# Chosen-token lists written by indirect stores to DRAM, and early sums tied to a point of each half tile

## The chip, the cores and the metric

The kernel runs on one core of a Trainium2 chip. Five engines of the core run their own instruction streams in order: TensorE (PE in the profile, with PEld for its weight loads), VectorE (DVE), ScalarE (ACT), GpSimd (POOL) and SyncE (SP). SP issues most DMAs, POOL issues the indirect ones. An instruction that waits holds up all that stand behind it on the same engine, and so does a DMA that cannot yet be issued. The metric is the device time of one execution in microseconds (us); before the change it is 5029.28 us, the median of three runs (5026.99 to 5029.7).

## What is computed

```
x = x + ssm(layernorm(x))                       # 8 sequences of 2048 tokens, 512 wide
h = layernorm(x)
light = window attention over h                 # 64-token windows and their neighbours
s   = h . routing_token                         # one score per token, for queries and for keys
scores = coordinate_descent(s, 50 iterations)   # then top_k: 512 queries, 1024 keys a sequence
out = null_q everywhere; out[chosen queries] = heavy attention(chosen queries, chosen keys)
x = x + light + out
```

The choice of tokens is a list of row numbers and one weight for each entry: per sequence 512 query rows and 1024 key rows. The order inside a list is not in the result, only which row goes with which weight.

## The kernel before

**Three phases.** `ssm_phase` computes the state space model and stores its result to DRAM (`ys`). `light_phase` makes x1 (input plus that result), its norm, the window attention, and the routing scores. `heavy_phase` gathers the chosen rows with indirect DMAs and does the full attention over them. The chip is most of the time in the last two.

**Tiling of the light phase.** There are 128 tiles of 128 tokens (`NTT`), taken in 32 macro tiles of four (`NMT`, index n). Each tile is done in two half tiles of four heads, so `steps()` (lines 930 to 1000) runs 256 half-tile steps s. A step turns the weights of step s (`turned`, L885 to L892), finishes the tile before it (`finish`, L912 to L919) or runs a piece of the projections of the next macro tile (`front`, L790 to L808), weighs step s+2 (`weigh`, L859 to L875), and sums (`sum_up`, L903 to L907). PE's order is that of the program text (a manual schedule). The other engines' orders are made by a scheduler from the dependences and the order of recording; `tc.issue_after(i)` keeps what is recorded under it from being placed before instruction i.

**Finishing a tile.** DVE adds the projection and x1 into `row` (L914); SP stores `row` to `base` (L916); POOL adds the null query into `nul` (L918); SP stores `nul` to the output (L919). `row` and `nul` have two buffers each, so the row of tile t can be written only when POOL has read the row of tile t-2 and SP's store of it is done. x1 for a tile comes back from DRAM as `x1r` (L944), three buffers, issued by SP two tiles ahead. POOL also copies the halo of `xt` (L766) and `kk` (L785) once per macro tile.

**Sums and scores.** `total` loads x (L673), gathers the state space result in reverse order with an indirect DMA on POOL (L678), adds (L682) and takes the mean and variance. `score` stores x1 (L703) and forms the two routing scores (L709); `scale` multiplies them by the root (L719). For the first 16 macro tiles (`FIRST`) this is done in `rows(n)`, two macro tiles ahead of use; for the last 16 in `early(n)`, spread over the first 16 macro tiles as `sooner`, one piece at the end of every step, with no anchor.

**Routing.** `route` is a generator per group of four sequences. `between` advances each running one by one piece, twice a step, with its instructions anchored behind those of the step. It does 49 iterations of the descent, 33 halvings of a threshold, and a running count, which gives each chosen token its place in its list (`r_u`) and leaves 1,000,000 (`SKIP`) for the others. Then the list is built by products: for each of the eight lists of the group, DVE makes selection matrices (`r_ge`, `r_at`, `r_dat`, and `r_one` at L591), PE multiplies them (L597, 128x128 by 128x16, four in a piece) and DVE adds up (`r_acc`, L600 and L602) and writes the row numbers `ix` and the weights `wt`. Group 0 starts at n = 15, group 1 at n = 16. The heavy phase reads group 0's lists first and group 1's half way.

Of the kernel before, what the change touches and what calls it, by code (L numbers as in the profile page):

```python
# [17 lines left out]
P = 128  # L18
# [362 lines left out]
N_BISECT = 33  # L381
SKIP = 1.0e6
NLT = NKV // P


def route_consts(tc, k, pool):
    nc = tc.nc

    k.before = pool.tile([P, P], F32, name="before", tag="before")
    nc.gpsimd.memset(k.before, 1.0)  # L390
    sv = k.before.rearrange("p (r t) -> p r t", t=NCK)
    nc.gpsimd.affine_select(sv, sv, [[-NCK, P // NCK], [0, NCK]], ALU.is_ge, 0.0, base=0,
                            channel_multiplier=1)
# [12 lines left out]
    k.na1 = pool.tile([P, 1], F32, name="na1", tag="na1")  # L406
    k.num = pool.tile([P, 1], F32, name="num", tag="num")
    for r, (keff, n) in enumerate(((KEFF_Q, NQ), (KEFF_KV, NKV))):
        s = slice(64 * r, 64 * r + 64)
        nc.vector.memset(k.logk[s], math.log(keff))  # L410

        nc.vector.memset(k.na1[s], math.log(L) - math.log(keff))
        nc.vector.memset(k.num[s], float(n))

    k.tiles = pool.tile([P, NLT + 1], F32, name="tiles", tag="tiles")
    nc.gpsimd.iota(k.tiles, [[P, NLT + 1]], base=0, channel_multiplier=0,
                   allow_small_or_imprecise_dtypes=True)
    k.places = pool.tile([P, P], F32, name="places", tag="places")
    nc.gpsimd.iota(k.places, [[1, P]], base=0, channel_multiplier=0,
                   allow_small_or_imprecise_dtypes=True)  # L420


def route(tc, k, ps, gi, ix, wt):

# [143 lines left out]

    NA = 4
    for rb in range(2 * GB):
        cs = slice(rb * NCK, (rb + 1) * NCK)
        rs = slice(rb % GB * NCK, (rb % GB + 1) * NCK)
        ge = pool.tile([P, NCK, NLT + 1], F32, name="r_ge", tag=f"r_ge{gi}", bufs=1)
        nc.vector.tensor_tensor(ge, pos[:, cs].unsqueeze(2).to_broadcast([P, NCK, NLT + 1]),
                                k.tiles.unsqueeze(1).to_broadcast([P, NCK, NLT + 1]), ALU.is_ge)
        at = pool.tile([P, NCK], F32, name="r_at", tag=f"r_at{gi}", bufs=1)  # L580
        nc.vector.reduce_sum(at, ge[:, :, 1:], axis=AX.X)
        nc.vector.scalar_tensor_tensor(at, at, -float(P), pos[:, cs], ALU.mult, ALU.add)
        dat = pool.tile([P, NCK, 2, NLT], F32, name="r_dat", tag=f"r_dat{gi}", bufs=1)
        nc.vector.tensor_tensor(dat[:, :, 1], ge[:, :, :NLT], ge[:, :, 1:], ALU.subtract)
        for e, src in ((0, rows[:, rs]), (1, wts[:, cs])):
            nc.vector.tensor_tensor(dat[:, :, e], dat[:, :, 1],
                                    src.unsqueeze(2).to_broadcast([P, NCK, NLT]), ALU.mult)
        acc = pool.tile([P, 2, NLT], F32, name="r_acc", tag=f"r_acc{gi}", bufs=2)
        for i in range(0, NCK, NA):
            one = pool.tile([P, NA, P], F32, name="r_one", tag=f"r_one{gi}", bufs=1)  # L590
            nc.vector.tensor_tensor(one, at[:, i : i + NA].unsqueeze(2).to_broadcast([P, NA, P]),  # L591
                                    k.places.unsqueeze(1).to_broadcast([P, NA, P]),
                                    ALU.is_equal)
            yield
            pa = pst((P, 2, NLT))
            for j in range(NA):
                nc.tensor.matmul(pa, one[:, j, :], dat[:, i + j], start=j == 0,  # L597
                                 stop=j == NA - 1)
            if i == 0:
                nc.vector.tensor_copy(acc, pa)  # L600
            else:
                nc.vector.tensor_tensor(acc, acc, pa, ALU.add)  # L602
        nc.vector.tensor_copy(ix[:, rb], acc[:, 0])
        nc.vector.tensor_copy(wt[:, rb], acc[:, 1])

# [7 lines left out]
def light_phase(tc, k, ps, wp, args, x, ys, x1, base, out, between, after):  # L613
# [6 lines left out]
    with ExitStack() as ctx:  # L620
        k.pool = ctx.enter_context(tc.tile_pool(name="route", bufs=1, reuse_waits="tile"))
        route_consts(tc, k, k.pool)
        scores = k.scores = [k.pool.tile([P, P], F32, name=f"sc{i}", tag=f"sc{i}")
                             for i in range(B // GB)]
        cst = ctx.enter_context(tc.tile_pool(name="li_c", bufs=1, reuse_waits="tile"))
# [43 lines left out]
        def total(n, i):  # L669

            c = n * MT + i
            t = sb.tile([P, D], F32, name="x1t", tag="x1t", bufs=6)
            nc.sync.dma_start(t, xf[c * P : (c + 1) * P, :])  # L673
            y = sb.tile([P, D], F32, name="yt", tag="yt", bufs=2)
            b, r = divmod(c, NCK)

            with tc.issue_after(came["pow"].ins) if n == 1 else nullcontext():
                nc.gpsimd.indirect_dma_start(  # L678
                    out=y, out_offset=None, in_=ys[b],
                    in_offset=bass.IndirectOffsetOnAxis(ap=back[:, r : r + 1], axis=0),  # L680
                    bounds_check=L - 1, oob_is_err=False)
            nc.vector.tensor_add(t, t, y)  # L682
            st = sb.tile([P, 6], F32, name="st", tag="st", bufs=3)
            nc.vector.bn_stats(st, t)
            nc.vector.bn_aggr(mv[:, c, :], st)
            return t

        def roots(n):
# [8 lines left out]
                                    ALU.mult, ALU.add)  # L697
            came["pow"] = nc.gpsimd.tensor_tensor(rc[:, :, ns], rc[:, :, ns], k.halves, ALU.pow)

        def score(n, i, t):  # L700

            r0 = (n * MT + i) * P
            nc.sync.dma_start(x1[r0 : r0 + P, :], t)  # L703
# [9 lines left out]
        def scale(n):  # L713

            b, c = divmod(n * MT, NCK)
            for r in range(2):
                col = (r * GB + b % GB) * NCK + c
                sc = scores[b // GB][:, col : col + MT]
                nc.vector.tensor_tensor(sc, sc, rc[:, 0, n * MT : (n + 1) * MT], ALU.mult)  # L719

        def early(n):

            for i in range(MT):
                t = total(n, i)
                yield
                score(n, i, t)
                yield
            roots(n)
            scale(n)

        def rows(n):
# [11 lines left out]
            for i in range(MT):  # L743
                c = n * MT + i
                if n >= FIRST:
                    t = sb.tile([P, D], F32, name="x1t", tag="x1t", bufs=6)
                    nc.sync.dma_start(t, x1[c * P : (c + 1) * P, :])
                    ts.append(t)
                nc.vector.tensor_scalar(z[:, i, :], ts[i], mv[:, c, 0:1], rc[:, 1, c : c + 1],
                                        ALU.subtract, ALU.mult)  # L750
                if n < FIRST:
                    score(n, i, ts[i])
                yield
            if n < FIRST:
                scale(n)
            it["z"] = z

# [175 lines left out]
        def steps():  # L933
# [20 lines left out]

            for s in range(2):
                weigh(s)
            ahead = beyond = turning = sooner = None
            done = None
            for s in range(nst):
                t, half = divmod(s, 2)  # L960
# [378 lines left out]
def model(ctx, tc, ins, out, debug=None):  # L1339
# [9 lines left out]
    if debug is not None:  # L1349
# [6 lines left out]
    wp = ctx.enter_context(tc.tile_pool(name="wts", bufs=1, reuse_waits="tile"))  # L1356
    lists = [[rpool.tile([P, 2 * GB, NLT], dt, name=f"{n}{i}", tag=f"{n}{i}")
              for n, dt in (("ix", U32), ("wt", F32))] for i in range(B // GB)]
    running = []

    def between(anchors=None, group=None):


        if group is not None:
            running.append(route(tc, k, ps, group, *lists[group]))
            return
        for r in list(running):
            with ExitStack() as held:
# [46 lines left out]
```

## Time and profile before

| what | value |
|---|---|
| median of three runs | 5029.28 us |
| the profiled execution's own time | 5022.05 us |
| its span | 5020.4 us |
| mean granted TensorE clock | 0.972 |
| busy share PE / DVE / ACT / POOL | 91% / 59% / 38% / 17% |
| state space phase | to about 541 us |
| light phase | to about 3305 us |
| heavy phase | from there to the end |

The span is the time between the first and the last instruction of one profiled execution. A group's row in the profile names the line, the engine, the tiles written and read, the shape and how often it occurs; then the busy time in us and the mean of one in ns; then the engine's idle time just before the group and what ended it. A busy row of PE counts matmuls whose ends are modelled, so rows of different groups can overlap and their sum can exceed the time. One float32 matmul of the program stands in the profile as two.

### The profile page before, as it was taken

The page shows a single profiled execution, that of the slowest core. Times are in us where ns is not written, and L with a number is a line of the kernel's source. Part 1 is how long each engine was busy: PE and PEld are TensorE (multiplying, and loading weights), DVE is VectorE, ACT ScalarE, POOL GpSimd, SP SyncE. Part 2 cuts the span into 40 slices and gives each one's busy share as a digit, 9 for nine tenths or more (in the row PEclk, how much of TensorE's full clock was granted, in tenths as well). Part 3 has the DMA queues.
Part 4 walks back from the last instruction along what each step waited for, and adds up shares of the span by engine and source line. Part 5 has one row for each costly group of instructions (what it writes and reads, how often), then busy time and mean ns, then how long its engine had stood idle before and what let it go on. Part 6 is the DMA issues. An engine that isn't in the chain of part 4 may idle for free. (4 is left out here: it accounts for less than half of the span.)

```text
span 5020.4 us, 75066 instructions
## 1 busy us (share of the span) xinstructions
PE 4572.1 (91%) x28808; PEld 2684.0 (53%) x28808; DVE 2946.8 (59%) x7240; ACT 1892.5 (38%) x5077; POOL 852.8 (17%) x878
## 2 busy tenths in 40 slices
PE   0867689999999999999999999989999999999987
PEld 0656445555555555555555565545555555555554
DVE  8566586767676655666677655444444444444443
ACT  6967223333333333444333222323333333333333
POOL 6344231222222110000000000020111011110000
PEclk9988799999999999999999999999999999999998
DMA  7487642334333321111111101220000000010000
GB/s 258 145 234 234 207 156 93 129 101 137 102 125 105 103 76 47 55 53 55 49 53 51 45 32 37 59 87 22 30 26 30 18 26 30 26 30 18 20 9 13
DMA packets 286344, 392.48 MB, mean 78 GB/s; under 512 B 38304, under 2 KB 152224, under 8 KB 285984
## 3 DMA queue, kind: packets, MB, share of 16 engines
q1 hardware_dynamic: 241056, 278.59, 16.9%
q0 software_dynamic: 29840, 101.73, 6.6%
q10 hardware_dynamic: 15088, 7.34, 0.5%
q8 instruction: 227, 3.72, 0.3%
q14 instruction: 133, 1.09, 0.1%
HBM read 244.46 MB, written 143.13 MB: 77 GB/s over the span
## 5 line engine op out<-in xcount | busy, mean ns | idle before, releaser
L790 PE MATMUL pp<-xt,wqkv 128*128 128x512 f32 x2048 | 952.8, 609 | 11.7 <-DVE kk L795 11.7
L790 PEld LDWEIGHTS pp<-xt,wqkv 128*128 128x128 f32 x2048 | 375.5, 193 | 421.0 <-issue 407.3
L869 ACT ACTIVATE pe<-sim,nb 128x256 f32<-128x256 f32 x1024 | 471.1, 473 | 239.2 <-DVE nb L864 163.1
L1215 DVE TENSOR_REDUCE mx<-sim 128x1 f32<-128x1024 f32 x256 | 312.8, 1222 | 339.8 <-PE sim L1209 192.7
L803 PE MATMUL pv<-wqkv,xt 128*128 128x512 f32 x1032 | 472.6, 601 | 0.0
L912 PE MATMUL pr<-wo,ot 128*128 128x512 f32 x1024 | 460.8, 593 | 0.0
L1219 ACT ACTIVATE pe<-sim,nb 128x1024 f32<-128x1024 f32 x256 | 285.3, 1114 | 457.0 <-DVE nb L1216 444.2
L907 ACT COPY ot<-po 128x256 f32<-128x256 f32 x256 | 95.3, 372 | 918.8 <-PE po L903 917.5
L864 DVE TENSOR_REDUCE nb<-sim 128x4 f32<-128x1024 f32 x256 | 311.7, 1217 | 137.1 <-PE sim L859 130.3
L918 POOL TENSOR_TENSOR nul<-row,nq 128x512 f32<-128x512 f32 x128 | 168.7, 1318 | 1256.6 <-DVE row L914 948.9
L1284 PE MATMUL pt<-ident,pe 128*128 128x128 f32 x2048 | 283.1, 282 | 87.9 <-ACT pe L1219 61.3
L1158 PE MATMUL pp<-xt,wa 128*128 128x512 f32 x768 | 351.8, 602 | 4.4 <-DVE kk L1163 4.4
L1284 PEld LDWEIGHTS pt<-ident,pe 128*128 128x128 f32 x2048 | 232.0, 144 | 171.2 <-ACT pe L1219 88.2
L1287 DVE COPY pw<-pt 128x512 f32<-128x512 f32 x256 | 175.5, 685 | 242.6 <-PE pt L1284 242.1
L885 PEld LDWEIGHTS pt<-ident,pe 128*128 128x128 f32 x2048 | 239.8, 141 | 132.0 <-issue 131.1
L903 PE MATMUL po<-pw,v 128*64 128x128 f32 x4096 | 292.1, 285 | 15.0 <-DVE pw L892 14.6
L875 DVE TENSOR_SCALAR pe<-pe,rec 128x256 f32<-128x256 f32 x1024 | 300.3, 355 | 6.0
L803 PEld LDWEIGHTS pv<-wqkv,xt 128*128 128x128 f32 x1032 | 185.6, 189 | 204.7 <-issue 200.1
L912 PEld LDWEIGHTS pr<-wo,ot 128*128 128x128 f32 x1024 | 184.6, 190 | 183.8 <-issue 183.3
L1289 ACT COPY pw<-pt 128x512 f32<-128x512 f32 x256 | 149.8, 585 | 350.5 <-PE pt L1284 350.5
L903 PEld LDWEIGHTS po<-pw,v 128*64 128x64 f32 x4096 | 224.4, 139 | 84.3 <-issue 48.9
L1209 PE MATMUL sim<-kk,q 64*128 64x512 f32 x1024 | 267.0, 641 | 0.0
(241 smaller groups left out, 7019.1 us busy)
## 6 DMA issues: line engine op xcount, KB each, us to landing
xin<-in_L_attn_x_dram SPq DMA_DIRECT2D x32, 1024.0 KB, 5.6
toe<-kd SPq DMA_DIRECT2D x64, 512.0 KB, 3.9
x1t<-in_L_attn_x_dram SPq DMA_DIRECT2D x128, 256.0 KB, 2.9
x<-x1t SPq DMA_DIRECT2D x128, 256.0 KB, 2.2
x1r<-x SPq DMA_DIRECT2D x128, 256.0 KB, 2.8
base<-row SPq DMA_DIRECT2D x128, 256.0 KB, 2.1
out_dram<-nul SPq DMA_DIRECT2D x128, 256.0 KB, 2.1
y<-xb POOLq DMA_DIRECT2D x25, 1024.0 KB, 11.0
```

The lines of the kernel that those rows point to most:

```text
L790: nc.tensor.matmul(pp, wqkv[:, c, j * D + f * P : j * D + (f + 1) * P], xt[:, c, WIN:], start=c == 0, stop=c == NC - 1)
L803: nc.tensor.matmul(pv[0:m], xt[:, c, s * P : s * P + m], wqkv[:, c, 2 * D :], start=c == 0, stop=c == NC - 1)
L864: dve = nc.vector.reduce_max(nb, sim.rearrange("p a b c -> p (a b) c"), axis=AX.X, negate=True)
L869: act = nc.scalar.activation(pe[:, i, :], sim[:, i // 2, i % 2, :], AF.Exp, bias=nb[:, i : i + 1], accum_out=sums[:, i : i + 1])
L875: nc.vector.tensor_scalar(pe[:, i, :], pe[:, i, :], rec[:, i : i + 1], None, ALU.mult)
L903: nc.tensor.matmul(po[64 * par : 64 * par + 64, pr, :], vs[kb][:, h * DH : (h + 1) * DH], self.pw[pr][:, par, kb, :], start=kb == 0, stop= ...
L912: nc.tensor.matmul(pr, ot[:, c, :], wo[:, c, :], start=c == 0, stop=c == NC - 1)
L1158: nc.tensor.matmul(pp, w[:, f * P : (f + 1) * P], xt[:, c, :], start=c == 0, stop=c == NC - 1)
L1209: nc.tensor.matmul(sim[:, par, ms], q[rows_, f, self.qs], kk[rows_, f, ms], start=True, stop=True)
L1215: nc.vector.reduce_max(mx, sim[:, par, :], axis=AX.X, negate=True)
L1219: nc.scalar.activation(pe, sim[:, par, :], AF.Exp, bias=self.nb[:, h : h + 1], accum_out=self.sums[:, h : h + 1])
L1284: nc.tensor.transpose(pt[:, i, :], pes[half][:, kb * P : (kb + 1) * P], k.ident)
```

## The change

**Lists.** The products are gone. Each list position gets the list's first slot added (`k.first`), is cast to an integer (`r_to`), and row number and weight are put side by side (`r_pair`). For each of the 128 columns (eight lists by 16 tiles) an indirect store on POOL writes 128 pairs of 8 bytes to DRAM at their places; places beyond the bound are dropped. The columns go in turn to four DRAM copies of the lists (`NFL`), which were filled with zeros at the start of the light phase. SP then loads the four copies of each list back (`r_got`), and DVE sums them (`r_one`) and writes `ix` and `wt`. The generator yields after every second store. Group 0 starts one macro tile sooner, at n = 14.

**Early sums.** The pieces of `sooner` stand under `issue_after` of the first instruction that `turned` returned, in the middle of the step. The x1 store is taken out of `score` and issued ahead of it. The scores of the first two macro tiles are left out of `rows` and done by `later` at n = 2 and 3, from x1 loaded again. `scale` runs on POOL in place of DVE. `x1t` has seven buffers in place of six, `yt` three in place of two.

```diff
+NFL = 4
...
-    k.tiles = pool.tile([P, NLT + 1], F32, name="tiles", tag="tiles")
...
+    k.first = pool.tile([P, 2 * GB, NCK], F32, name="first", tag="first")
+    nc.gpsimd.iota(k.first, [[NKV, 2 * GB], [0, NCK]], base=0, channel_multiplier=0,
...
-    NA = 4
-    for rb in range(2 * GB):
...
-            one = pool.tile([P, NA, P], F32, name="r_one", tag=f"r_one{gi}", bufs=1)
-            nc.vector.tensor_tensor(one, at[:, i : i + NA].unsqueeze(2).to_broadcast([P, NA, P]),
...
+    nc.vector.tensor_tensor(pos, pos, k.first, ALU.add)
+    nc.vector.tensor_copy(to, pos)
+    nc.vector.tensor_copy(pair[:, :, 1], wts)
+    for r in range(2):
+        nc.vector.tensor_copy(pair[:, r * GB * NCK : (r + 1) * GB * NCK, 0], rows)
+    yield
+    for b in range(GB):
+        for rb, n in ((b, NQT), (GB + b, NLT)):
+            for c in range(rb * NCK, (rb + 1) * NCK):
+                nc.gpsimd.indirect_dma_start(
+                    out=flat[c % NFL], out_offset=bass.IndirectOffsetOnAxis(ap=to[:, c : c + 1],
+                                                                            axis=0),
+                    in_=pair[:, c, :], in_offset=None, bounds_check=2 * GB * NKV - 1,
+                    oob_is_err=False)
+                if c % 2:
+                    yield
+    for b in range(GB):
+        for rb, n in ((b, NQT), (GB + b, NLT)):
+            got = pool.tile([P, NFL, NLT, 2], F32, name="r_got", tag=f"r_got{gi}", bufs=2)
+            with nc.allow_non_contiguous_dma(reason="pairs"):
+                for i in range(NFL):
+                    nc.sync.dma_start(
+                        got[:, i, :n], flat[i][rb * NKV : rb * NKV + n * P, :].rearrange(
+                            "(t p) e -> p t e", p=P))
             yield
-            pa = pst((P, 2, NLT))
-            for j in range(NA):
-                nc.tensor.matmul(pa, one[:, j, :], dat[:, i + j], start=j == 0,
-                                 stop=j == NA - 1)
...
+            one = pool.tile([P, NLT, 2], F32, name="r_one", tag=f"r_one{gi}", bufs=2)
+            nc.vector.reduce_sum(one[:, :n], got[:, :, :n].rearrange("p i t e -> p t e i"),
+                                 axis=AX.X)
+            nc.vector.tensor_copy(ix[:, rb, :n], one[:, :n, 0])
+            nc.vector.tensor_copy(wt[:, rb, :n], one[:, :n, 1])
...
+        nil = k.pool.tile([P, GB * NKV * 2 // P], F32, name="nil", tag="nil")
+        nc.gpsimd.memset(nil, 0.0)
+        for t in [t for ts in k.flats for t in ts]:
+            for i in range(2):
+                nc.sync.dma_start(t[i * GB * NKV : (i + 1) * GB * NKV, :].rearrange(
+                    "(p n) e -> p (n e)", p=P), nil)
...
-            t = sb.tile([P, D], F32, name="x1t", tag="x1t", bufs=6)
+            t = sb.tile([P, D], F32, name="x1t", tag="x1t", bufs=7)
...
-            y = sb.tile([P, D], F32, name="yt", tag="yt", bufs=2)
+            y = sb.tile([P, D], F32, name="yt", tag="yt", bufs=3)
...
-                nc.vector.tensor_tensor(sc, sc, rc[:, 0, n * MT : (n + 1) * MT], ALU.mult)
+                nc.gpsimd.tensor_tensor(sc, sc, rc[:, 0, n * MT : (n + 1) * MT], ALU.mult)
...
                 t = total(n, i)
+                nc.sync.dma_start(place_of(n, i), t)
                 yield
                 score(n, i, t)
...
+        def later(n):
+
+            for i in range(MT):
+                score(n, i, fetched(n, i))
+                yield
             scale(n)
...
-                    if n == FIRST - 1:
+                    run(after_all)
+                    if n == FIRST - 2:
                         between(group=0)
...
+                    after_all = later(n - 2) if n in (2, 3) else None
...
+                with tc.issue_after(anchors[0].ins):
+                    run(sooner, 1)
+                    run(after_all, 1)
...
-                run(sooner, 1)
```

More of the change, by code (lines that the diff above doesn't have):

```diff
@@ L413, in route_consts, with route @@
         nc.vector.memset(k.num[s], float(n))
-    k.tiles = pool.tile([P, NLT + 1], F32, name="tiles", tag="tiles")
-    nc.gpsimd.iota(k.tiles, [[P, NLT + 1]], base=0, channel_multiplier=0,
+    k.first = pool.tile([P, 2 * GB, NCK], F32, name="first", tag="first")
+    nc.gpsimd.iota(k.first, [[NKV, 2 * GB], [0, NCK]], base=0, channel_multiplier=0,
                    allow_small_or_imprecise_dtypes=True)
[L418 to L423, printed above, removed]
+    k.first = k.first.rearrange("p r c -> p (r c)")
+def route(tc, k, ps, gi, flat, ix, wt):
     nc = tc.nc
@@ L569, in route @@
     nc.vector.tensor_copy(wts, pt)
-    NA = 4
-    for rb in range(2 * GB):
[L575 to L589, printed above, removed]
-            one = pool.tile([P, NA, P], F32, name="r_one", tag=f"r_one{gi}", bufs=1)
-            nc.vector.tensor_tensor(one, at[:, i : i + NA].unsqueeze(2).to_broadcast([P, NA, P]),
-                                    k.places.unsqueeze(1).to_broadcast([P, NA, P]),
-                                    ALU.is_equal)
-            yield
-            pa = pst((P, 2, NLT))
-            for j in range(NA):
-                nc.tensor.matmul(pa, one[:, j, :], dat[:, i + j], start=j == 0,
-                                 stop=j == NA - 1)
[L599 to L604, printed above, removed]
@@ new lines, in route @@
+    to = pool.tile([P, P], U32, name="r_to", tag=f"r_to{gi}", bufs=1)
+    pair = pool.tile([P, P, 2], F32, name="r_pair", tag=f"r_pair{gi}", bufs=1)
+    nc.vector.tensor_tensor(pos, pos, k.first, ALU.add)
[14 more added lines that the diff above has]
+                    yield
@@ L698, in roots, with place_of @@
             came["pow"] = nc.gpsimd.tensor_tensor(rc[:, :, ns], rc[:, :, ns], k.halves, ALU.pow)
+        def place_of(n, i):
+            r0 = (n * MT + i) * P
+            return x1[r0 : r0 + P, :]
         def score(n, i, t):
-            r0 = (n * MT + i) * P
-            nc.sync.dma_start(x1[r0 : r0 + P, :], t)
             b, c = divmod(n * MT + i, NCK)
@@ L728, in early, with fetched @@
             roots(n)
+            scale(n)
+        def fetched(n, i):
+            t = sb.tile([P, D], F32, name="x1t", tag="x1t", bufs=7)
+            nc.sync.dma_start(t, place_of(n, i))
+            return t
+        def later(n):
+            for i in range(MT):
+                score(n, i, fetched(n, i))
+                yield
             scale(n)
@@ L745, in rows @@
                 if n >= FIRST:
-                    t = sb.tile([P, D], F32, name="x1t", tag="x1t", bufs=6)
-                    nc.sync.dma_start(t, x1[c * P : (c + 1) * P, :])
-                    ts.append(t)
+                    ts.append(fetched(n, i))
                 nc.vector.tensor_scalar(z[:, i, :], ts[i], mv[:, c, 0:1], rc[:, 1, c : c + 1],
@@ L751, in rows @@
                 if n < FIRST:
+                    nc.sync.dma_start(place_of(n, i), ts[i])
+                if 2 <= n < FIRST:
                     score(n, i, ts[i])
                 yield
-            if n < FIRST:
+            if 2 <= n < FIRST:
                 scale(n)
@@ L956, in steps @@
                 weigh(s)
-            ahead = beyond = turning = sooner = None
+            ahead = beyond = turning = sooner = after_all = None
             done = None
@@ L1358, in model @@
               for n, dt in (("ix", U32), ("wt", F32))] for i in range(B // GB)]
+    flats = k.flats = [[dr.tile([2 * GB * NKV, 2], F32, name=f"list{g}{i}", tag=f"list{g}{i}")
+              for i in range(NFL)] for g in range(B // GB)]
     running = []
@@ L1364, in between @@
         if group is not None:
-            running.append(route(tc, k, ps, group, *lists[group]))
+            running.append(route(tc, k, ps, group, flats[group], *lists[group]))
             return
```

## The prediction

> **What bounds the kernel now.** I read the slices first, then the light phase by stretches, then the waits at its two ends.
>
> ```profile
> PE   0867689999999999999999999989999999999987
> DVE  8566586767676655666677655444444444444443
> POOL 6344231222222110000000000020111011110000
> PEclk9988799999999999999999999999999999999998
> ```
>
> From slice 5 on PE is busy nine tenths or more. POOL, which the change loads, is all but empty from slice 15 to 25. So what leaves PE there shortens the run, and what makes PE wait lengthens it.
>
> Next, time per tile in the light phase. A tile has four L912 matmuls, so eight records. The rows are windows: start:end, length, PE busy (count), PE weight loads, and in the whole-core rows DVE, ACT, POOL; then granted clock, DMA share and GB/s. First a stretch without products: whole core, then L912 alone. Then the same two for the stretch that has the products, and last the products (tile rps).
>
> ```profile
> 2100.00:2720.00 620.00, 618.25 (x3593) 333.99 (x3593) 431.69 (x1680) 243.45 (x879) 49.03 (x46) 1.00 0.16 54
> 2100.00:2720.00 620.00, 111.56 (x248) 44.70 (x248) 1.00 0.16 54
> 2720.00:3090.00 370.00, 357.25 (x2136) 224.30 (x2135) 228.13 (x633) 93.31 (x305) 23.00 (x24) 0.95 0.11 37
> 2720.00:3090.00 370.00, 50.38 (x112) 20.19 (x112) 0.95 0.11 37
> 2720.00:3090.00 370.00, 66.45 (x518) 66.39 (x518) 11.80 (x67) 0.95 0.11 37
> ```
>
> 248/8 = 31 tiles in 620 us is 20.0 us a tile. 112/8 = 14 tiles in 370 us is 26.4. The 90 us more are the products' 66, 12.75 us in which PE idles (370 - 357.25; 10.7 of it for r_one), and the rest a clock of 0.95.
>
> **Parts that save.** *Products out.* 14 tiles x (26.4 - 20.0) = **-90 us**, all on the path. DVE sheds 64 r_one (58.7 us) and some 50 us of small operations, and gains under 20 us; DVE isn't the bound there, so nothing more. Ends: -63 (the products with the overlap of modelled ends taken off) to -95.
>
> *The start of the light phase.*
>
> ```profile
> 577.29 4.25 PE L770 MATMUL pt<-ident,z 128*128 128x128 f32 x16 [36.12 <-DVE z L749]
> 606.96 16.62 PE L790 MATMUL pp<-xt,wqkv 128*128 128x512 f32 x32 [11.68 <-DVE kk L795]
> 647.88 1.11 PE L770 MATMUL pt<-ident,z 128*128 128x128 f32 x4 [9.25 <-DVE xt L772]
> ```
>
> In brackets is PE's wait. The 36 us end when x1t has landed; its loads follow the last stores of y, one about every 6 us, and the built order leaves that chain alone. What changes is DVE: eight scores of 0.75 + 0.08 us are gone from between the last landing (570.8) and z (576.7), which can take 2 us off. The kk copy at 606 stands behind two sums whose loads SP issues at 600, and in the new order behind three, but with SP's x1 stores ahead: about -3, then +2 for the next copy. The 9.25 us are DVE busy with early scores, all moved away: -9. Together **-11 us** (0 to -25). The eight scores come back at n = 2 and 3, with eight loads of 256 KB; DVE is at 213 of 300 us there, which hides their 13 us. If it were full, +13.
>
> *Costed at nothing.* The 16 zero fills stand on SP among the last toe loads: at 0.33 us an issue 5 us, and their 2048 packets of 256 bytes over 16 engines, at the mean 56 ns a packet that the queue table gives, 7 us. The last toe was issued 25 us before its use. Without that cover, +7. `scale` on POOL: 64 x 0.20 us (row L231, same shape) for 64 x 0.155 on DVE; POOL has 200 of 300 us free. More buffers: in 760 to 2700 PE waits only 19 us in all, so the tie of the early sums can save at most that, or lose as much if a late gather holds DVE: 0, ends -15 and +15.
>
> **The part that costs: 256 indirect stores on POOL.** The trace before has POOL's indirect DMAs, five gathers back to back and a store followed by a gather (start, duration, idle before):
>
> ```profile
> 3306.41 1.00 POOL L1085 DMA_INDIRECT xg<-x,ix  x1 [0.30 <-issue]
> 3307.72 1.00 POOL L1085 DMA_INDIRECT xg<-x,ix  x1 [0.31 <-issue]
> ...
> 3474.42 1.05 POOL L1273 DMA_INDIRECT out_dram<-row,ix  x1 [10.20 <-DVE row L1271]
> 3475.78 1.03 POOL L1085 DMA_INDIRECT bg<-base,ix  x1 [0.31 <-issue]
> ```
>
> From start to start 1.31 us for a gather, 1.36 for a store, which lands 2.8 us after its issue. These move 2 KB a row and the new ones 8 bytes, but each has 128 rows. I take 1.36; ends 1.0 (dropped rows cost less, no gap) and 1.7.
>
> Here a rule speaks differently. The Trainium skill, "DMA: Bandwidth & Descriptors", section on the anatomy of one DMA (SWDGE path), puts sequencer dispatch at about 50 ns, calls descriptor generation "small, variable", and gives most of a fixed 2 us to the write receipt. By it POOL would be nearly free during a store, and only the chain of four lists (each store waits for the one four before it) would pace them: four in 2 us, 64 us a group. The row says POOL is held 1.05 + 0.30 us. I go by the row.
>
> The generator hands out two stores a piece, four a step of 10 us, which would be harmless: 5.4 of 10 us. But the built order doesn't keep that pace on POOL. Group 0's 128 stores stand in one block behind the nul of one tile, call it a, with only these between: 15 stores, kk, 15, nul of a+1, 29, xt, 8, nul of a+2, 35, nul of a+3, 26, nul of a+4. Group 1's block, ten tiles later: 31, nul, 34, nul, 18, kk, 16, nul, 28, xt, 1, nul. So four tiles of nul (80 us) hold 174 us of stores, and nul runs late. The row of tile t waits for the nul of t-2 (two buffers), and DVE stands in that wait with all behind it: the reduce of the next half tile, hence ACT's exp, hence PE.
>
> With row a at 0, the stores start at 2.2 us (row 0.7, four small route operations to 1.9, nul). nul takes 1.27, kk 0.82, xt 0.40, gaps 0.2. End of nul: a+1 at 2.2 + 30 x 1.36 + 2.5 = 45.5; a+2 at 45.5 + 37 x 1.36 + 2.1 = 97.9; a+3 at 147.0; a+4 at 183.8. Without a stall row a+k comes at 20k. Row a+4 (80) waits to 98, row a+5 (118) to 147, row a+6 (167) to 184. SP adds 4: `r_got` loads wait there for the last store's landing (183.8) and stand ahead of the base store of a+4, which row a+6 also waits for; four issues and a landing of 2.0 make 188. So row a+6 is 188 - 120 = 68 us late. When DVE stops, PE still has sim 0.9, sum 1.1, a projection 3.6 and transposes 1.0, 6.6 us. **61 us a group, +122.** At 1.0 us a store: row a+6 at 142, 22 late, +16 a group. At 1.7: +105 a group.
>
> *Clock after the stalls.* Windows at the start of the light phase grant 0.50 in 560 to 580, where PE idles to 577, and 0.93 in 580 to 600, 20 x 0.07 = 1.4 us lost. The skill's "TensorE: Matmul & The Clock Gate" (Part 1) says half rate until about 3.4 us of activity, 1.7 us a restart. Six stalls: **+9**, by the rule +10.
>
> *Reading back.* Group 0's loads in pairs of buffers cost DVE about 7 us a turn (issue 4 x 0.4 to 1.5, landing about 4), hidden by DVE's free half; at the very end group 1's eight sums stand within two or three tiles: **+5** (0 to 20). SP issues 64 loads, some 30 us in all.
>
> **Sum.** -90 - 11 + 122 + 9 + 5 = +35 on the profiled 5022.05 us (span 5020.4 and 1.65 around it), 5057. The profiled run lies 7.2 under the median of runs, so +35 on 5029.28: **5064 us**.
>
> **Rivals.** (A) *The stores drain fast*: 1.0 us each or less. The stall is 2 x 16 and 4 of clock; -90 - 11 + 36 + 5 = -60: **4969**. Four of ten or more places are dropped (SKIP), which speaks for it; the fixed 1.0 us of every indirect DMA speaks against. It decides under about 1.22 us a store, where the stalls equal the savings. This one ends on the other side. (B) *The stores are slower than the row*: 8-byte writes land late, and each waits for the one four back; beyond a landing of about 5.4 us the landing paces POOL. At 7 us, 1.75 a store: +111 a group, 5064 + 100 = **5164**. For it: nothing here shows an 8-byte scatter. Against: 2.8 us for 256 KB. (C) *A wash*: the nul queue backs up but half the products' saving is lost to a clock that stays low: or stores of 1.22 us: **5029**. That the tie doesn't pace anything is part of the main case.
>
> **How the numbers follow.** Main case 0.60, own range 5035 to 5100 (1.28 to 1.45 us a store is +-22; the other ends +-15). A 0.24, B 0.10, C 0.06. The range 4978 to 5115 leaves out half of A's spread and all but the edge of B's. 0.2% is 10 us, about what a measurement of this kernel can tell from none. Faster: A, and a little of C, 0.25. Same: half of C and the main case's lower edge, 0.07. Slower 0.68.
>
> **What would show it.** Right: the rps group gone and 20.0 us a tile outside the blocks; store-to-store near 1.36 us on POOL; three waits of DVE's row for POOL's nul in each block, some 18, 29 and 20 us, with PE idle behind them, its share falling in slices 21 to 25 where it was whole; x1 loads on SP late; the 9 us wait for xt gone. Wrong: stores at 1.0 us or spread among the nul, DVE's row waiting for PE alone; or idle of PE in the first half of the light phase, from gathers that hold DVE.

## The result, and the profile after

The changed kernel takes 5091.75 us, the median of four runs (5086.41 to 5095.47), against 5028.14 us before: 1.0126 times as long, with a 95% interval of 1.0108 to 1.0143. It is 63.6 us slower. The forecast, made from a median of three runs before (5029.28), was 35 us slower (5064), with a range of 4978 to 5115.

The slices of the changed kernel, each 127.3 us, counted from 0 as in the prediction:

```profile
PE   0777699999999999999996886979999999999987
DVE  8576377776767666666773533444445444444443
POOL 6253222222222211000026263021011011110000
PEclk9988899999999999999998898999999999999998
```

From slice 5 on PE is whole up to slice 20. It drops to 6, 8, 8, 6 in slices 21 to 24, where POOL, empty before, rises to 6, 2, 6, 3. These are the two blocks of stores. (The 7 of slice 26 is the start of the heavy phase, which the kernel before has too, in its slice 26 as an 8.) The groups name the wait; the first row is of the kernel before, the other two of the changed one. After the count and the bar stand busy time, mean of one in ns, and the idle time before it with what ended it:

```profile
L790 PE MATMUL pp<-xt,wqkv 128*128 128x512 f32 x2048 | 952.8, 609 | 11.7 <-DVE kk L795 11.7
L810 PE MATMUL pp<-xt,wqkv 128*128 128x512 f32 x2048 | 951.7, 608 | 120.4 <-DVE row L934 107.2
L583 POOL DMA_INDIRECT list<-r_pair,r_to x256 | 250.8, 980 | 118.9 <-issue 67.6 <-DMA list<-r_pair,r_to 45.7 <-DVE r_mid L513 2.8
```

In this group PE waits 107 us for DVE's row; before, it waited 11.7 us in all. Next, what DVE waited for between 2300 and 3400 us (sum, times, longest):

```profile
DVE row L934 <- POOL nul L938: 117.7, 4, 37.8
DVE row L934 <- PE pr L932: 68.0, 40, 4.4
DVE row L934 <- DMA base<-row: 65.4, 2, 37.0
```

Six long waits, four for a late nul and two for a late store of base. Both come from one thing, which POOL's and SP's timelines of the first block show. On POOL, nul stands among stores; on SP, the base store stands behind the loads that read the lists back:

```profile
2741.78 1.28 POOL L938 TENSOR_TENSOR nul<-row,nq 128x512 f32<-128x512 f32 x1
2743.23 0.99 POOL L583 DMA_INDIRECT list<-r_pair,r_to  x1 [0.17 <-issue]
2744.53 0.97 POOL L583 DMA_INDIRECT list<-r_pair,r_to  x1 [0.30 <-issue]
2747.18 0.97 POOL L583 DMA_INDIRECT list<-r_pair,r_to  x1 [1.68 <-DMA list<-r_pair,r_to]
...
2794.18 1.28 POOL L938 TENSOR_TENSOR nul<-row,nq 128x512 f32<-128x512 f32 x1
...
2830.94 1.28 POOL L938 TENSOR_TENSOR nul<-row,nq 128x512 f32<-128x512 f32 x1
```

```profile
2795.49 0.34 SPq L939 DMA_DIRECT2D out_dram<-nul  x1
2829.70 9.07 SPq L595 DMA_DIRECT2D r_got<-list  x8
2838.87 0.52 SPq L936 DMA_DIRECT2D base<-row  x1
```

The rows follow at once (DVE's timeline):

```profile
2795.50 0.69 DVE L934 TENSOR_TENSOR row<-pr,x1r 128x512 f32<-128x512 f32 x1 [37.77 <-POOL nul L938]
2841.47 0.69 DVE L934 TENSOR_TENSOR row<-pr,x1r 128x512 f32<-128x512 f32 x1 [28.39 <-DMA base<-row]
```

One row starts 0.04 us after the nul of two tiles before has ended (2794.18 + 1.28); the next one waits for the base store that SP could issue at 2838.87 only. A store takes 0.97 us and 0.30 us of gap, and now and then more, where it waits for the landing of the store four before it.

**Where the 70.7 us of the profiled execution went** (its span, 5020.4 to 5091.1). The start of each tile's row on DVE is read in both timelines; the differences at tiles 0, 96, 116 and 127 split the run:

| stretch | before | after | difference |
|---|---|---|---|
| to the row of tile 0 | 682.9 | 671.7 | -11.2 |
| tile 0 to 96 | 1951.7 | 1964.7 | +13.0 |
| tile 96 to 116 | 495.4 | 557.9 | +62.5 |
| tile 116 to 127 | 172.8 | 178.6 | +5.8 |
| from there to the end of the span | 1717.6 | 1718.2 | +0.6 |

Outside the blocks the pace is 20.0 us a tile: between 2100 and 2620 us the changed kernel has 208 records of L932, eight a tile, in 520 us. So 20 tiles without products and stalls would be 400 us: the products took 95 us of the kernel before, and the blocks of stores cost 158 us, 79 a group.

### The profile page after: what moved, and what is told of

Read it like the earlier page. It is cut to its first block, busy times and chain, and to the rows that moved or that the text cites. A ratio compares the mean times of both kernels' runs of the same rounds, so it can differ in the third digit from the quotient of the medians.

```text
span 5091.1 us, 74548 instructions
## 1 busy us (share of the span) xinstructions
PE 4515.4 (89%) x28296; PEld 2618.6 (51%) x28296; DVE 2880.2 (57%) x6978; ACT 1893.7 (37%) x5077; POOL 1106.3 (22%) x1198
## 5 line engine op out<-in xcount | busy, mean ns | idle before, releaser
L932 PE MATMUL pr<-wo,ot 128*128 128x512 f32 x1024 | 461.1, 593 | 0.0
L1308 PE MATMUL pt<-ident,pe 128*128 128x128 f32 x2048 | 283.4, 282 | 87.9 <-ACT pe L1243 61.1
L905 PE MATMUL pt<-ident,pe 128*128 128x128 f32 x2048 | 268.4, 274 | 31.3 <-DVE xt L792 31.3
L932 PEld LDWEIGHTS pr<-wo,ot 128*128 128x128 f32 x1024 | 184.8, 191 | 184.0 <-issue 182.8
L583 POOL DMA_INDIRECT list<-r_pair,r_to x256 | 250.8, 980 | 118.9 <-issue 67.6
```

The source lines that it names most:

```text
L905: nc.tensor.transpose(pt[:, par, kb, :], self.pe[:, 2 * par + pr, kb * P : (kb + 1) * P], k.ident)
L932: nc.tensor.matmul(pr, ot[:, c, :], wo[:, c, :], start=c == 0, stop=c == NC - 1)
L1308: nc.tensor.transpose(pt[:, i, :], pes[half][:, kb * P : (kb + 1) * P], k.ident)
```

## The experiments

All times are medians; the ratio is to the kernel before, run on the same chip. Four kernels were run once, for their traces. The three with dropped rows leave the lists empty, so only their light phase is read; the kernel with half of the stores leaves out half of the list entries. The numbers that tell most are the rows of the light phase again. The column "chip" will matter below; for the kernel before and the changed one it is not on record.

| kernel | chip | us | ratio (95%) | row of tile 96, to before | tile 96 to 116 |
|---|---|---|---|---|---|
| before | - | 5028.14 | | | 495.4 |
| changed | - | 5091.75 | 1.0126 (1.0108 to 1.0143) | +1.8 | 557.9 |
| lists alone | 12 | 5111.79 | 1.0182 (1.0147 to 1.0218) | +6.3 | 570.4 |
| early sums alone | 12 | 5049.91 | 1.0040 (1.0025 to 1.0056) | +19.3 | 497.0 |
| half of the stores | 12 | 5067.15 | 1.0076 (1.0056 to 1.0096) | -2.1 | 521.2 |
| stores tied to nul | 12 | 4991.28 | 0.9926 (0.9907 to 0.9945) | +2.2 | 459.2 |
| tied, and in turn | 3 | 4949.71 | 0.9846 (0.9830 to 0.9863) | +2.6 | 407.5 |
| paced by DVE | 3 | 4955.76 | 0.9851 (0.9835 to 0.9868) | +7.3 | 420.7 |
| tied, rows dropped | 3 | 4978.90, one run | | +0.6 | 412.2 |
| early sums untied | 3 | 5083.95, one run | | -15.8 | 565.9 |
| in turn, untied | 9 | 4931.31 | 0.9792 (0.9775 to 0.9810) | -14.8 | 415.1 |
| in turn, untied, reading tied | 9 | 4938.46 | 0.9809 (0.9794 to 0.9825) | -17.7 | 414.0 |
| changed, rows dropped | 9 | 5069.49, one run | | -1.2 | 513.7 |
| half, rows dropped | 9 | 4986.95, one run | | +4.7 | 415.5 |

**The two parts of the change alone.** In the first kernel the hunks of the early sums are left out, in the second those of the lists (and the buffers stay at six and two, as the products' tiles leave no room for more):

```diff
 # lists alone
-                with tc.issue_after(anchors[0].ins):
-                    run(sooner, 1)
-                    run(after_all, 1)
+                run(sooner, 1)          # at the end of the step, as before
 # early sums alone
-    for b in range(GB): ... indirect_dma_start ... r_got
+    for rb in range(2 * GB): ... r_ge, r_at, r_dat, r_one, rps ...
```

> Only the lists are changed; the early sums, their buffers and the scores stay as before. Theory (the whole loss is the two blocks of stores on POOL): the profile of the changed kernel lost 158 us in 20 tiles there and saved 96, so +62, 5090 us, within 8; rows 97 to 116 as late as in the changed kernel. Rival (the tie of the early sums keeps its 11 us of gain and the lists are dearer than they look, or the early sums are to blame for a part): more than 5105, or less than 5070.

> Only the early sums are changed (tied, x1 store ahead of the score, first eight scores done later, scale on POOL); lists by products as before, and six and two buffers as before, since the products' tiles leave no room for more. Theory: 11 us are gained at the first tile and given back by tile 16, where DVE waits for gathers: 5028 us, within 6. Rival (the gain stays and something in the list part eats it): 5017 us.

Both came out some 20 us above the theory, 5112 in place of 5090 and 5050 in place of 5028. So the lists carry the loss, but the early sums are no wash: alone they lose 28 us between tile 0 (-8.5) and tile 96 (+19.3), and stay there. And the lists alone lose something that POOL's queue does not explain: the rows of tiles 97 and 98 are late already, by 10 and 2 us, when no nul is late. In that kernel ACT stood 142.3 us in ten waits of its copy ot (at most 55.6 us) that no instruction of the profile ended. The next run shows the same more plainly.

**Half of the stores.**

```diff
             for c in range(rb * NCK, (rb + 1) * NCK):
+                if c % 2:
+                    yield
+                    continue
                 nc.gpsimd.indirect_dma_start(
-                    out=flat[c % NFL], ...
+                    out=flat[c // 2 % NFL], ...
```

> The changed kernel with every second store left out, so half of the list entries stay zero. Theory: the blocks are 64 x 1.42 = 91 us long, the row of the fourth tile after the block's start waits for 17 us and SP's loads add some 9; about 20 us a group in place of 79: 5092 - 118 = 4974 us, within 15. Rival (a fixed price for each block, or for the reading back): over 5030 us. Rival (price by the store, with nothing that covers it): half of 158 is left, 5013 us.

5067 us: a clear miss of both expectations that count by the store (4974 and 5013), and nearest to "a fixed price for a block". The stall moved forward: the rows of tiles 97, 98 and 99 came 49.4, 30.7 and 34.6 us apart. The queue does not explain it: when the row of tile 97 came, POOL had issued 30 of the 64 stores and was itself waiting for that row. PE's timeline there, with no wait that the profile can name:

```profile
2709.05 0.45 PE L924 MATMUL po<-pw,v 128*64 128x128 f32 x1 [1.01 <-issue]
2709.75 0.37 PE L924 MATMUL po<-pw,v 128*64 128x128 f32 x1 [0.25 <-issue]
2710.47 0.67 PE L924 MATMUL po<-pw,v 128*64 128x128 f32 x2 [0.35 <-issue]
2711.89 0.37 PE L924 MATMUL po<-pw,v 128*64 128x128 f32 x1 [0.75 <-issue]
2712.61 0.45 PE L924 MATMUL po<-pw,v 128*64 128x128 f32 x1 [0.35 <-issue]
```

and ACT, which reads that po:

```profile
2704.80 0.59 ACT L911 COPY pw<-pt 128x512 f32<-128x512 f32 x1 [0.87 <-PE sim L880]
2733.11 0.37 ACT L928 COPY ot<-po 128x256 f32<-128x256 f32 x1 [27.72 <-remote]
```

po was done at 2713.1, and ACT began at 2733.11, 20 us later; DVE's reduce (L885) waited in the same way for 16.1 us until 2729.47. The last store went out at 2729.68. PE sends its matmuls one at a time, 0.7 or 1.4 us apart, where sixteen of them take 1.1 us elsewhere. So a second cause exists: in this kernel, while stores run, signals between engines come late. The forecast had no term for it, and it had to be separated from the queue.

**Moving the stores, not taking them away.** In the changed kernel the pieces of the route stand behind anchors that are DVE's and ACT's instructions, and POOL's order was not held by them. Here each store stands behind a POOL instruction:

```diff
-            nc.gpsimd.tensor_tensor(nul, row, nq, ALU.add)
+            k.nul = nc.gpsimd.tensor_tensor(nul, row, nq, ALU.add)
...
+                with tc.issue_after(k.nul.ins):
                     nc.gpsimd.indirect_dma_start(out=flat[c % NFL], ...)
```

> The changed kernel with each indirect store put behind the nul of the tile last finished, on POOL itself: eight stores between two nul, sixteen where the two groups overlap. All 256 stores remain. Theory (it is the place in POOL's order that costs): in the overlap 16 x 1.3 + 1.3 + 0.6 = 22.7 us of POOL work stand in a tile of 20 us, some 15 us late over six tiles, elsewhere nothing: 5092 - 158 + 15 = 4949 us, within 20. Rival (the stores slow DVE, SP or PE wherever they stand): 5040 to 5090 us.

4991 us, 100 us under the changed kernel with the same 256 stores: the place in POOL's order is most of the loss. But it is 42 us more than the theory said. Group 0 alone, eight stores behind each nul, costs next to nothing (tile 97 to 107 in 206.8 us, ten tiles). In the overlap, sixteen a tile, tiles 107 to 113 come up to 29.5 us apart, not 22.7. ACT's waits between 2850 and 3010 us:

```profile
ACT ot L928 <- remote: 74.3, 5, 18.6
ACT ot L928 <- PE po L924: 17.4, 5, 4.0
```

These are the late signals again. In each of the five waits ACT starts 1.4 to 3.5 us after the last store of the run has started (2886.84 and 2890.29 in the first), long after PE's po. With eight stores it is seen too, but small: po is done at 2691.43 and ACT starts at 2693.66. The next runs ask what makes the signals late: the length of an unbroken run of stores, or the rows that are written.

**No more than a dozen in a row.** Besides the tie:

```diff
+    while gi and k.storing:      # group 1 waits until group 0 has issued its last store
+        yield
...
-                if c % 2:
+                if c % 5 in (2, 4):
                     yield
+    k.storing = False
```

> As the run with stores tied to nul, but group 1 waits with its stores until group 0 has issued all of its own, and each group issues ten a tile: runs of 9 to 12 stores behind each nul, never 16. Theory 1 (only POOL's queue costs, and it has 10 x 1.28 + 1.9 = 14.7 us of work in a tile of 20): the 56 us that the overlap lost come back, 4991 - 56 = 4935 us, within 10. Theory 2 (an unbroken run of stores of more than some 10 us makes other engines' signals late, 9.2 us for 16 stores, nothing for 8): some 2.3 us in each of 26 tiles, 60 us, 4990 us; over 4960 speaks for it.

4949.7 us, 15 over theory 1, which allowed 10, and 40 under theory 2. Tile 96 to 116 takes 407.5 us, where the plain pace would need 400: the stall is gone. In ACT's waits over all these tiles there is none without a releaser:

```profile
ACT ot L932 <- PE po L928: 203.1, 55, 7.3
```

So nine to twelve stores behind each nul are harmless here. That sixteen are not is not shown by this pair alone, as the two kernels ran on different chips. The untied kernel, on chip 3 like this one and also without late signals, has the two blocks and takes 565.9 us for the same tiles: on one chip, the same 256 written stores cost 166 us in two blocks and 8 us in tens. POOL itself waited 52.2 us for landings in this run, more than in the changed kernel, and nobody behind it cared. What is left above the theory is mostly the last five tiles, which lost 8 us.

> As the run in turn, but the pairs of five columns are written by DVE in the step that issues them, so POOL gets five stores every half tile (6.4 us of 10), and the reading back is tied to SP's store of nul, six pieces after the last store. Theory 1 and theory 2 both: no stall is left, 5092 - 158 = 4934 us and a few us for the waits of POOL on DVE, 4940 us within 10. If it is over 4960, neither the queue nor the length of the runs explains the loss.

```diff
+        for j, c in enumerate(cs[i : i + PER]):      # PER = 5, written in the step that stores them
+            nc.vector.tensor_copy(pair[:, j, 1:2], wts[:, c : c + 1])
+            nc.vector.tensor_copy(pair[:, j, 0:1], rows[:, r0 : r0 + 1])
```

4956 us, 6 over the upper end that both theories gave, and no better than the run in turn. Five stores at a time buy nothing over ten. 13 us more than in the run in turn went between tiles 96 and 116, in tiles 112 and 113 (29.4 and 29.2 us). There DVE's sums of group 0's lists stand in its queue ahead of their loads, as they do in the run in turn (30.4 us in twelve waits):

```profile
DVE r_one L609 <- DMA r_got<-list: 33.5, 8, 7.6
```

In the changed kernel DVE has no such wait before tile 116. So the forecast's "hidden" for group 0's loads held there, and does not hold in kernels in which the stall is gone.

**Nothing written.** 1,000,000 is added to every place, so all rows are beyond the bound:

```diff
     nc.vector.tensor_tensor(pos, pos, k.first, ALU.add)
+    nc.vector.tensor_scalar(pos, pos, SKIP, None, ALU.add)
```

> As the run with stores tied to nul, with 1,000,000 added to every place, so that every row of every store is beyond the bound and nothing is written (the lists stay zero, and the heavy phase gathers row 0 again and again; so only the rows of the light phase are compared, tile 107 to 113 of them). If the 8-byte writes are to blame for the late signals, a tile with sixteen stores takes about 22.7 us; if POOL's own work for a store is, about 29 us as with the writes.

Tiles 107 to 114 take 147.9 us, 21.1 each; with the writes it was 191.5. (Tile 113, 27.9 us, has a wait of 13.2 us of DVE's list sum for its load.) POOL's stores last as long as before (0.98 us and 0.30 of gap in the middle), so the time they take on POOL does not by itself disturb the others. In windows 2860 to 3000 us, length, then PE busy (records), weight loads, DVE, ACT, POOL, granted clock: first tied, then tied with the rows dropped.

```profile
2860.00:3000.00 140.00, 112.42 (x589) 57.66 (x587) 44.23 (x93) 32.43 (x109) 83.46 (x84) 0.90 0.11 31
```

```profile
2860.00:3000.00 140.00, 134.11 (x793) 72.93 (x792) 63.07 (x132) 44.90 (x145) 109.52 (x109) 0.98 0.21 44
```

POOL is busier in the second, and PE is busy 134 of 140 us. As the expectation puts it, the writes would be to blame. But the two runs differ in the chip as well; more on this below.

> The changed kernel with 1,000,000 added to every place, so that nothing is written (lists stay zero; only the rows of the light phase are read, tile 96 to 116, 558 us in the changed kernel and 400 without a stall). POOL keeps the same 256 stores at 1.28 us in the same two blocks. Theory (POOL's queue, as predicted from durations alone): the waits for landing, some 20 us a group, are gone, the rest stays: 510 us within 12. Rival (the written rows cause the stall, by late signals): under 440 us.

> The run with half of the stores, and nothing written either (tile 96 to 116: 521 us with the writes). Theory (half the queue leaves about 20 us a group, and the rest of what that run lost, some 80 us, comes from the writes, which make signals late): 440 us within 15. Rival (a block has a price of its own): 500 to 525 us.

513.7 us and 415.5 us. In the changed kernel the queue is nearly everything: with nothing written the same two blocks still cost 114 us, 57 a group in place of 79, and the 22 us between match the waits for landing (45.7 us over both groups in the group's row above, 1.1 us here). DVE's waits without the writes, 2620 to 3200 us:

```profile
DVE row L935 <- POOL nul L939: 85.0, 4, 31.4
...
DVE row L935 <- DMA base<-row: 54.2, 2, 31.1
```

The same six waits, a quarter shorter. With half of the stores, 106 of the 121 us above 400 are gone, and the queue of 64 stores is worth 8 us a group, even less than the 20 that were worked out.

Whether the writes make the signals late, these runs cannot say. The kernels with late signals (lists alone, half of the stores, tied) all ran on chip 12. In the eight kernels that ran on chips 3 and 9, ACT has no wait without a releaser between 2600 and 3290 us, and DVE none over 2.4 us: not with the rows dropped, not in turn, and not in the untied kernel, which writes the same two blocks of 128 stores as the lists alone. Stores are needed, as the early sums alone, on chip 12 with no store, show none. But no kernel with stores ran on two chips, so the chip, the written rows and the length of a run are not told apart. What may be put down to the late signals (106 us in the kernel with half of the stores, 44 us in tiles 107 to 114 of the tied one) is no part of the changed kernel's loss: its trace has no such wait.

**The tie of the early sums.**

```diff
-                with tc.issue_after(anchors[0].ins):
-                    run(sooner, 1)
-                    run(after_all, 1)
+                run(after_all, 1)
...
                 run(beyond, 2)
+                run(sooner, 1)
```

> The changed kernel with the early sums at the end of the step and without the tie, as before the change; x1 store, later scores, scale on POOL and buffers stay changed. Read at the row of tile 96 in its trace. Theory (the tie makes DVE wait for gathers at tiles 8 to 16, and takes back what the start gained): row of tile 96 some 9 us earlier than in the kernel before. Rival (the eight later scores take it back): 2 us later than before, as in the changed kernel.

The row of tile 96 comes 15.8 us earlier than before the change, not 1.8 later: the tie costs 17.6 us, and the eight later scores nothing that can be seen. (On the same chip, the run in turn with the tie stands at +2.6.) DVE's wait between 760 and 1800 us, before and in the changed kernel; it is 0.2 us in the untied one:

```profile
DVE x1t L682 <- DMA yt<-y,back: 2.6, 5, 0.9
DVE x1t L687 <- DMA yt<-y,back: 103.9, 43, 5.2
```

and the windows of that stretch, changed kernel first, untied second (columns as above):

```profile
760.00:1800.00 1040.00, 1013.61 (x5829) 544.26 (x5828) 733.76 (x1696) 339.12 (x1113) 251.79 (x253) 1.00 0.36 116
```

```profile
760.00:1800.00 1040.00, 1031.94 (x5966) 554.10 (x5965) 729.28 (x1678) 345.25 (x1134) 249.93 (x242) 1.00 0.35 113
```

PE is busy 18 us longer in the same 1040 us. With the tie, DVE's sum is queued at a point of the step where its gather has not landed, and all of DVE waits with it.

**The best of it together.** The run in turn with the sums untied, once as it is and once with the reading back tied to SP's store of nul:

> The run in turn (ten stores a tile behind nul, group 1 after group 0) with the early sums at the end of the step and without the tie, as they stood before the change. If the two parts are independent: 4950 us of the run in turn, less the 17.6 us that the row of tile 96 stood earlier without the tie: 4932 us, within 8. If the gain without the tie is taken back where the stores are: 4950 us.

> As the run in turn and untied, with the reading back of the lists tied to SP's store of nul and six pieces after the last store, so that SP's base stores do not stand behind loads that wait for a landing. In the run in turn the last five tiles lost 8 us. If SP's loads caused that: 4 to 8 us under the run in turn and untied. If DVE's sums of the lists did: the same time.

```diff
+            k.based = nc.sync.dma_start(out[r0 : r0 + P, :], nul)
...
+            with nc.allow_non_contiguous_dma(reason="pairs"), tc.issue_after(k.based.ins):
                 for i in range(NFL):
                     nc.sync.dma_start(got[:, i, :n], ...)
```

4931.3 us, 0.9792 of the kernel before (0.9775 to 0.9810), as the sum of the parts said (4932). It is 105 us under the kernel before on that chip and beats both kernels. The tied reading makes no difference: 4938.5 us with an overlapping interval, and tiles 116 to 127 take 180.7 us against 180.5. So SP's loads ahead of the base stores are not what slows the last tiles. DVE's sums of the lists wait there, 8.6 us in five waits as it is and 7.2 us in four with the reading tied; that they are all of the 8 us is not shown.

## Why the prediction was right, and which terms were off

The direction, the mechanism and the range held. Point by point, by the steps of the sum, on the profiled execution:

| step | forecast | measured |
|---|---|---|
| products out | -90 (ends -63, -95) | -95 |
| start of the light phase | -11 | -11.2 |
| early sums, more buffers ("0, ends -15 and +15") | 0 | +13.0 |
| stalls of the two groups, and the clock after them | +122 and +9 | +158 |
| reading back at the end | +5 | +5.8 |
| sum | +35 | +70.7 (with +0.6 after the light phase) |

*Products out.* The 20.0 us a tile came back. Right. (One reading of the slices was off: PE's slice 5 before is an 8; the nine tenths begin at slice 6.)

*The start.* The 9.25 us wait for xt is gone, the wait for z ends 3.6 us earlier (577.29 to 573.73), and the row of tile 0 is 11.2 us earlier. Right, in size as well (the step's own terms, -2, -3, +2 and -9, add to -12). In the changed kernel the gain does not last, which the step did not say.

*Costed at nothing.* "The tie of the early sums can save at most that, or lose as much if a late gather holds DVE: 0, ends -15 and +15." The mechanism was named and the value taken from the middle; it was near the upper end. The tie alone is worth 17.6 us, and what the step took for a cover (PE waits only 19 us there, DVE has room) is no cover: DVE was not short of time, it stood behind one instruction, 103.9 us in 43 waits. The eight scores at n = 2 and 3, by contrast, were hidden as stated.

*The stores.* The price of one: 1.36 us was taken from the row of a 2 KB store; it was 0.97 + 0.30, some 1.28 us from start to start, for rows of 8 bytes and for rows that are dropped. The rule of the Trainium skill, "DMA: Bandwidth & Descriptors" (anatomy of one DMA, SWDGE path), has a dispatch of about 50 ns and a small, variable descriptor time; read as "POOL is nearly free" it would have made rival A, and it was rightly passed over for the row. Rival B's wait for landing exists beside it: 45.7 us in 36 of 256 stores, 23 us a group. So the first block was longer and not shorter: its last nul ended 195.8 us after row a (2830.94 + 1.28 - 2636.43) in place of 183.8; 10 us less for the issue, 23 more for the landings.

*SP behind the last store.* "Four issues and a landing", 4 us: it was eight loads in 9.07 us ahead of the base store, 9.3 us from the end of nul to the row. That is 5 of the 17 us by which row a+6 was later than forecast (205.0 after row a, forecast 188, due at 120); the other 12 are the later nul. The 85 us less what PE still had to do, some 6 us as forecast, agree with the 79 us that a group cost. The three waits of the first block were 24, 32 and 26 us of extra tile time (44.0, 52.4 and 46.0 less 20) in place of 18, 29 and 20. The clock after the stalls is inside these: 0.86 granted on the mean in 2636 to 2878. What each restart cost was not measured; the 1.7 us that the prediction puts beside its own 1.4 is an estimate, from the 3.4 us at half rate of the Trainium skill's "TensorE: Matmul & The Clock Gate" (Part 1).

*The term that failed most* is thus the stall, 131 forecast with its clock and 158 measured: right mechanism, mis-sized by the landings and by SP. With +13 for the tie and 5 more saved by the products, these make the 36 us. The experiment with the rows dropped measures the forecast's own case, POOL's queue with no landing to wait for: 57 us a group with its clock, where the sum had 61 and 4.5 of clock; at 1.28 us a store that sum gives some 55, an estimate.

*The rivals.* By the forecast's sum, stores below 1.22 us would have turned the sign. The issue at 1.28 is close to that point, closer than the forecast thought; the landings took it away again. None of the rivals had signals that come late. The changed kernel was spared them; the same two blocks with the lists alone, on chip 12, were not (570.4 us in place of 557.9).

## What to carry to other kernels

An order written for one engine does not hold another: before work is spread over steps, look in the built order whether each engine that issues it has an anchor of its own, and count what stands between two instructions that others wait for. The same 256 stores cost 158 us in two blocks and 8 us in tens behind each nul. When such a stall is gone, the next wait shows: here DVE's list sums, queued ahead of their loads. And a queued instruction whose data are on the way is worse than a late one: the sums tied ahead of their gathers lost 17.6 us on an engine with 29% of its time free in that stretch (733.76 us busy of 1040).

## What the runs showed of the hardware

While indirect stores of 8-byte rows run back to back, the signals between the other engines can be late. In the tied kernel, with sixteen stores in 20 us (2048 list places), ACT began 10 to 14 us after PE's result was done; with blocks of 64 it waited up to 27.7 us, with blocks of 128 up to 55.6 us. PE's matmuls went out singly there, 0.7 us apart (seen in the blocks of 64). These three kernels ran on one chip. Eight others with stores, on two other chips, show nothing of it, with 9 to 12 stores behind each nul, with two blocks of 128, and with all rows dropped. So stores can go with late signals and need not; what makes the difference, and by which path, is open. The same kernel run on several chips would be the next test.

A row beyond the bound costs POOL what a written one does: 0.98 us for a store of 128 dropped rows, 0.97 for one of 128 rows of which some are kept. It costs next to nothing in landing: 1.1 us of waits over 256 stores with all rows dropped, 45.7 us with the rows written.
